# First chunks of a hop moved ahead of the last projection, and fifteen of 21 row gathers instead of ten, in a two-layer graph network on one core

## Chip, cores and metric

The kernel runs on one core of one Trainium2 chip. The metric is the device time of one launch in microseconds (us). A core has a matrix engine (PE, with its weight loads shown as PEld), a vector engine (DVE), a scalar engine (ACT), a general engine (POOL) and a queue that only starts transfers (SP). POOL starts the indirect transfers, the gathers; ACT and SP start plain ones. All numbers are float32.

## What is computed

Shapes: x is 8 batches of 2048 nodes with 128 features; adj, called R here, is a 2048 x 2048 matrix in which some 0.4% of the entries are not zero. Cut to what matters:

```python
# layer 0
res = si[:, :, None] + sj[:, None, :] + adj[None] * w_r + g_b
x = layernorm(x + einsum('bij,bjd->bid', res, x) @ weight + bias)
# layer 1: A1 = A2 = adj, so four hops come down to two
x1 = einsum('bnf,nw->bwf', x, adj)
x2 = 2 * einsum('bnf,nw->bwf', x1, adj) - x
y = relu(concat(x, x1, x2, x1, x2) @ Theta1 + bias)      # per node
x = layernorm(x + y)
```

In the kernel, layer 1 is a nested scheme over two "hops". With U = x Theta-part, hop 1 makes Y1 = x Theta-part + R^T U, and hop 2 makes x Theta-part + R^T Y1, then the relu, the residual and the layernorm.

## The kernel before, in words

**Tiling.** The 2048 nodes are 16 chunks of 128. A chunk's rows for all 8 batches are 128 x 1024 numbers (512 KB). Chunks 0 to 2 (`ND = 3`) are dense in layer 0: their product with R runs over all 16 chunks. The other 13 are sparse: of each the list of node rows that R really touches is known, and seven gathers (four lists for tiles of 32 columns, two for 64, one for 128) fetch those rows of the operand from DRAM into one of nine buffers `G`, which lie over the first nine tiles named Y (`fetch_lists`, line 736). `listed_rows` (line 886) multiplies them: eight matmuls with 32 columns of weights, four with 64 and two with 128, each written to the trace as two instructions, so 28 records a chunk. The matching rows of R are gathered by `gathers` (line 709): a small gather of 128 rows per list into one of four `stage` tiles, and `keep_r` (line 681) on DVE masks and packs a full stage. For chunks 0 to 2, which need lists in layer 1 alone, 21 such gathers (`dense_jobs = 7 * ND`) read adj itself: in the trace, `stage<-in_adj_dram,idr`. These come last in the list of jobs: four for each of chunks 0, 1, 2, then three for each.

**Order around the change.** The last part of layer 0 runs over the 13 sparse chunks, `seq` = 9 to 14, 3 to 8, and then 15 (`LAST`). In each turn PE does `listed_rows`, and `finish0` (line 379) on DVE and ACT adds the residual and takes the layernorm. `make_u` (line 388) of the chunk before runs meanwhile: 8 transposes on PE into PSUM, one copy of each half out of PSUM (DVE and ACT), 16 matmuls with Theta into two PSUM tiles of the tag "sm" (which has two buffers), two ACT copies, and one store of the chunk of U to `u_d`, issued by ACT. After the last chunk come the ten gathers of line 934, plain loads on SP (lines 937 and 939) and the `make_u` of chunk 15 (line 940). Then hop 1 starts.

**A hop** (line 942). `begin(n)` opens the accumulation of the hop's n-th chunk: 16 matmuls with x transposed (line 952) and two products with the chunk's diagonal block (line 878, 4 records), whose operand `own` and block `rd` SP has loaded. The accumulators are the two pairs of `bank` in turn, but each third chunk takes both "sm" tiles. `listed_rows` then adds the lists, `end` copies the result out and stores it. Three chunks are begun before the first `listed_rows`; from then on a chunk is begun two ahead. The first two chunks (`first`) gather from all of U but chunk 15, and take chunk 15's part by `block_rows` with a block `rl` that SP loads into the same three buffers as `rd`; the third and later gather from the whole of `u_d`. After the `listed_rows` of each chunk from the third on, hop 1 calls `gathers(2)`, until the 21 are done.

**What sets the order.** On PE, `in_order` ties each matmul of this part behind the one written before it. On POOL, `gather` (line 658) ties each gather behind the one before. SP's loads keep program order. So the order of the source is the order of these queues, and a gather that waits holds up all later ones.

Of the kernel before, what the change touches and what calls it, by code (L numbers as in the profile page):

```python
# [18 lines left out]
def kernel(  # L19
# [86 lines left out]
    def rows4(name):  # L106
        return w4.tile([P, B, D], F32, name=name, tag="w4")

    def flat(t):
        return t.rearrange("p b f -> p (b f)")  # L110
# [69 lines left out]
    def transpose4(srcs, name, t=None, dve=None, tie=None):  # L180

        pt = p_tr.tile([P, 4, P], F32, name=f"pt_{name}", tag="pt")
        for i, s in enumerate(srcs):
            mm = nc.tensor.transpose(pt[:, i, :], s, ident)  # L184
            if tie is not None:
                tie(mm)
        if t is None:
            t = trp.tile([P, 4, P], F32, name=f"tr_{name}", tag="tr")
        evict(t, pt, dve)
        return t  # L190
# [176 lines left out]
    def acc_pair():  # L367
        par[0] ^= 1
        return bank[2 * par[0]:2 * par[0] + 2]
# [18 lines left out]
    def make_u(c, z, xt, u=None, tie=None, mid=None):  # L388

        for h in range(2):  # L390
            transpose4([z[:, h * HB + i, :] for i in range(4)], f"p{c}_{h}",
                       xt[:, h * HB:(h + 1) * HB, :], tie=tie)
        if mid is not None:
            mid()
        if c < ND:
            nc.scalar.dma_start(out=xt_d[c], in_=flat(xt))
        if u is None:
            u = rows4(f"u{c}")
        for h in range(2):
            pp = p_sm.tile([P, HB, D], F32, name=f"pp{c}_{h}", tag="sm")  # L400
            for i in range(HB):
                mm = nc.tensor.matmul(  # L402
                    pp[:, i, :], xt[:, h * HB + i, :], th[:, 0, :], start=True, stop=True
                )
                if tie is not None:
                    tie(mm)
            nc.scalar.copy(u[:, h * HB:(h + 1) * HB, :], pp)  # L407
        nc.scalar.dma_start(out=u_d[c * P:(c + 1) * P, :], in_=flat(u))
# [262 lines left out]
    def gather_r(c, q, m, st, n):  # L671


        gather(
            st[:, n * m * P:(n + 1) * m * P],
            rr_d[c - ND].rearrange("n m f -> n (m f)") if m == 2 else adj128,
            idx if m == 2 else idr,
            4 * c + n if q else (LP + 2 * c, LP + 2 * c + 1, LF + c)[n], NX if m == 2 else N * NC,
        )
# [26 lines left out]
    dense_jobs = 7 * ND  # L706
    waiting = []

    def gathers(count, mm=None):

        for _ in range(count):
            if not jobs:
                break
            c, q, n = jobs.pop(0)
            if n == 0:
                if len(waiting) == 3:
                    keep_r(*waiting.pop(0))
                waiting.append((
                    c, q, int(c >= ND) + 1,
                    stages[:, turn[1] % 4 * BD:turn[1] % 4 * BD + BD + 4 * TW],  # L720
                ))
                turn[1] += 1
            gather_r(*waiting[-1], n)
            if mm is not None:
                tc.add_manual_dep(
                    order[-1].ins, mm.ins.name,
                    mybir.DependencyInfo(
                        mybir.DependencyClass.Sync, mybir.DependencyReason.DATA
                    ), reason="pace",
                )  # L730
# [78 lines left out]
    with nc.allow_non_contiguous_dma(reason="512-byte rows of blocks"):  # L809
        pending, accs, xr = None, acc0, load_x(0, "xr", nc.sync)  # L810
        for c in range(ND):
# [62 lines left out]
            pending, xr = (c, z, rows4(f"xt{c}")), xr1  # L874
# [8 lines left out]
    def own_rows(i, c, accs, start):  # L883
        block_rows(*own.pop((i, c)), accs, start, False)
# [19 lines left out]
    with nc.allow_non_contiguous_dma(reason="512-byte rows of a diagonal block"):  # L904
        def begin0(c):
            accs = acc_pair()
            own_rows(0, c, accs, True)
            if c in first:
                block_rows(Y[LAST], late0, accs, False, False)
            begun[c] = accs  # L910

        begun = {}
        xr = load_x(seq[0], "xs", nc.sync)
        begin0(seq[0])
        for c, c1 in zip(seq, seq[1:] + [None]):
            if c1 is not None:
                fetch_own(0, y0_d, c1)
                if c1 in first:
                    late0 = fetch_block(0, c1)
                xr1 = load_x(c1, "xs", nc.sync)  # L920
                put(c)
                while any(job[0] == c1 for job in jobs):
                    gathers(1)
            else:
                put(c)
            accs = begun.pop(c)
            if c == LAST:
                listed_rows(0, y0_d, c, accs, lambda: make_u(*pending, tie=in_order))
            else:
                listed_rows(0, y0_d, c, accs)  # L930
                make_u(*pending, *[None] * (4 - len(pending)), in_order, lambda: begin0(c1))
            z = finish0(c, accs, xr)
            if c == LAST:
                gathers(dense_jobs // 2)
            pending, xr = (c, z, x1t[c], held.get((1, c))), xr1
        for c in hops[:2]:
            fetch_own(1, u_d, c)
        for c in range(ND):
            fetch(xt_d[c], f"xt_{c}", x1t[c])
        make_u(*pending, tie=in_order)  # L940

        def hop(i, src):
            def begin(n):
                c = hops[n]
                if (i, c) not in own:
                    fetch_own(i, src, c)
                accs = acc_pair() if n % 3 < 2 else [
                    p_sm.tile([P, HB, D], F32, name=f"acc{i}_{c}_{h}", tag="sm") for h in range(2)
                ]
                for h in range(2):  # L950
                    for b in range(HB):
                        in_order(nc.tensor.matmul(  # L952
                            accs[h][:, b, :], x1t[c][:, h * HB + b, :], th[:, i, :],
                            start=(b == 0), stop=False, skip_group_check=True,
                        ))
                own_rows(i, c, accs, False)
                return accs

            def end(c, accs):
                z = held.get((i + 1, c)) if i == 1 else None  # L960
                if z is None:
                    z = rows4(f"z{i}_{c}")
                for h in range(2):
                    hs = slice(h * HB, (h + 1) * HB)
                    if i == 1:
                        evict(z[:, hs, :], accs[h], h == 1)
                        continue
                    pt = p_tr.tile([P, HB, P], F32, name=f"pt_r{c}_{h}", tag="pt")
                    for b in range(HB):
                        in_order(nc.tensor.transpose(pt[:, b, :], x1t[c][:, h * HB + b, :], ident))  # L970
                    nc.vector.tensor_add(z[:, hs, :], accs[h], b1bc.to_broadcast([P, HB, D]))
                    nc.vector.scalar_tensor_tensor(  # L972
                        z[:, hs, :], z[:, hs, :], 0.0, pt, op0=ALU.max, op1=ALU.add
                    )
                if i == 1:
                    nc.scalar.dma_start(out=y_d[c * P:(c + 1) * P, :], in_=flat(z))
                else:
                    layernorm(z, f"1_{c}")
                    nc.scalar.dma_start(
                        out=out[:, c * P:(c + 1) * P, :].rearrange("b p f -> p b f"), in_=z  # L980
                    )

            early = [begin(n) for n in range(3)]
            late = [fetch_block(i, c) for c in first]
            for n in range(2):
                listed_rows(i, src, hops[n], early[n])
            for n, c in enumerate(hops):
                if i == 1 and n == NC - 5:
                    while waiting:
                        keep_r(*waiting.pop(0))  # L990
                if n < 2:
                    block_rows(held[i, LAST], late[n], early[n], False, True)
                else:
                    listed_rows(i, src, c, early[n])
                    if i == 1:
                        gathers(2)
                if 1 <= n < NC - 2:
                    early.append(begin(n + 2))
                end(c, early[n])

        hop(1, u_d)
        hop(2, y_d)


# [86 lines left out]
```

## Time and profile before

| | us |
|---|---|
| runs | 852.25, 855.61, 860.12 |
| median | 855.61 |
| profiled execution, whole time | 867.91 |
| its span on the core | 866.1 |
| PE busy | 748.5 (86%) |
| POOL busy | 430.1 (50%) |
| DVE busy | 364.1 (42%) |
| ACT busy | 175.1 (20%) |
| moved by the transfers | 269.19 MB, mean 311 GB/s |

The span lies 1.8 us below its execution's own time, and that execution is 12.3 us over the median of the three runs. In the trace, layer 0 ends and hop 1 begins between about 462 and 490 us, hop 1 lasts to about 685 us, and hop 2 to the end. The page's row of DMA rates gives the share of each 1/40 of the span (21.65 us); the slices in which this border falls show 259 and 280 GB/s, those of the later part of hop 1 up to 394.

### The profile page before, as it was taken

How to read it: one execution, taken by the hardware profiler on the slowest of the kernel's cores; microseconds unless marked ns; L12 is line 12 of the kernel's file. 1: busy time of each engine (PE TensorE's matmuls, PEld its weight loads, DVE VectorE, ACT ScalarE, POOL GpSimd, SP SyncE). 2: the span in 40 equal slices, each digit the busy share in tenths (PEclk: the TensorE clock that was granted, in tenths of full speed). 3: DMA queues.
4: the chain of work that ended last, by engine and by line, in shares of the span. 5: the costliest groups of instructions: out<-in, count | busy, mean ns of one | idle time of the engine just before them, and what ended most of it. 6: DMA issues, size and time to landing. Idle time of an engine off the chain costs nothing.

```text
span 866.1 us, 10670 instructions
## 1 busy us (share of the span) xinstructions
PE 748.5 (86%) x3546; PEld 373.8 (43%) x3546; DVE 364.1 (42%) x1062; ACT 175.1 (20%) x428; POOL 430.1 (50%) x438
## 2 busy tenths in 40 slices
PE   5899999998829778498996987989999899999994
PEld 4666665643324333153344442333343444445541
DVE  5555667769523335155353010000100046555666
ACT  3665664010011212021222000000000002011111
POOL 0000000277466676657675456766655656566660
PEclk9999999999869998799998999999999999999998
DMA  8699997799968889979997889999998989999994
GB/s 283 194 306 309 342 303 215 231 373 398 287 212 264 268 274 322 368 250 344 342 363 259 280 314 349 315 341 394 383 365 307 322 290 372 350 341 354 342 350 155
DMA packets 177548, 269.19 MB, mean 311 GB/s; under 512 B 17698, under 2 KB 127701, under 8 KB 175438
## 3 DMA queue, kind: packets, MB, share of 16 engines
q0 software_dynamic: 50400, 151.21, 49.0%
q1 hardware_dynamic: 103900, 90.02, 32.0%
q10 hardware_dynamic: 23186, 27.20, 8.8%
q8 instruction: 30, 0.49, 0.2%
q14 instruction: 32, 0.26, 0.1%
HBM read 246.75 MB, written 62.55 MB: 357 GB/s over the span
## 4 chain that ended last, share of the span: by engine, by line
PE 53%; DMA 19%; issue 10%; another core or an unknown queue 8%; POOL 3%; DVE 3%; ACT 2%; POOLq 1%; SPq 0%; DVEq 0%; ACTq 0%
PE acc L894 19%; DMA Y<-u_d,idx 9%; DMA Y<-y_d,idx 9%; PE acc L862 7%; PE acc L878 5%; PE acc L342 4%; PE acc L332 4%; PE acc L952 3%; POOL Y L659 3%; PE pt_a L184 2%; PE pp L402 2%; DMA rc<-in_adj_dram 1%; PE pt_x L184 1%; PE pt_r L970 1%
## 5 line engine op out<-in xcount | busy, mean ns | idle before, releaser
L659 POOL DMA_INDIRECT Y<-y_d,idx x203 | 201.8, 994 | 134.7 <-PE acc L894 72.4
L894 PE MATMUL acc<-Y,rc 128*32 128x512 f32 (+2 forms) x896 | 222.3, 612 | 21.9 <-DMA Y<-u_d,idx 11.7
L659 POOL DMA_INDIRECT stage<-rr_d,idx x91 | 94.2, 1035 | 199.8 <-PE rank_c L514 164.4
L659 POOL DMA_INDIRECT Y<-u_d,idx x112 | 111.4, 994 | 69.8 <-PE acc L894 35.5
L894 PEld LDWEIGHTS acc<-Y,rc 128*32 128x32 f32 (+2 forms) x896 | 59.5, 129 | 174.5 <-issue 107.0
L894 PE MATMUL acc<-Y,rct 128*32 128x512 f32 (+2 forms) x364 | 106.2, 621 | 18.6 <-issue 14.0
L878 PE MATMUL acc<-Y,rd 128*128 128x512 f32 x148 | 70.0, 594 | 0.8 <-issue 0.8
L894 PEld LDWEIGHTS acc<-Y,rct 128*32 128x32 f32 (+2 forms) x364 | 25.5, 129 | 90.4 <-issue 67.5
L862 PE MATMUL acc<-Y,wide 128*128 128x512 f32 x128 | 59.9, 620 | 4.3 <-issue 4.3
L383 DVE TENSOR_TENSOR xs<-acc,xs 128x512 f32<-128x512 f32 x26 | 17.8, 684 | 103.8 <-PE acc L894 59.8
L176 DVE COPY z<-acc 128x512 f32<-128x512 f32 x9 | 6.2, 692 | 115.7 <-issue 41.0
L219 ACT ACTIVATE st<-st,epst 128x8 f32<-128x8 f32 x32 | 10.0, 311 | 210.1 <-DVE st L218 112.8
L184 PE MATMUL pt_a<-ident,rc 128*128 128x128 f32 x256 | 37.6, 282 | 6.4 <-DMA rc<-in_adj_dram 6.0
L972 DVE SCALAR_TENSOR_TENSOR z<-z,pt_r 128x512 f32<-128x512 f32 x32 | 20.5, 684 | 47.0 <-PE acc L894 28.5
L862 PEld LDWEIGHTS acc<-Y,wide 128*128 128x128 f32 x128 | 24.7, 199 | 34.5 <-issue 34.4
L311 DVE TENSOR_REDUCE stage<-rct 128x64 f32<-128x2048 f32 x13 | 29.7, 2286 | 23.1 <-ACT rct L178 23.1
L332 PE MATMUL acc<-wx,tr_x 128*128 128x130 f32 x256 | 36.5, 286 | 3.2 <-ACT tr_x L178 2.8
L303 DVE TENSOR_REDUCE rc<-rc 128x64 f32<-128x2048 f32 x16 | 36.5, 2278 | 6.3 <-DMA rc<-in_adj_dram 6.3
L332 PEld LDWEIGHTS acc<-wx,tr_x 128*128 128x128 f32 x256 | 32.8, 194 | 13.4 <-ACT tr_x L178 5.9
L184 PEld LDWEIGHTS pt_a<-ident,rc 128*128 128x128 f32 x256 | 30.9, 145 | 16.3 <-issue 14.7
L342 PE MATMUL acc<-Y,wide 128*128 128x512 f32 x64 | 36.0, 645 | 1.7 <-ACT Y L336 0.5
L407 ACT COPY u<-pp 128x512 f32<-128x512 f32 x30 | 17.5, 585 | 98.3 <-PE acc L894 58.7
(221 smaller groups left out, 895.2 us busy)
## 6 DMA issues: line engine op xcount, KB each, us to landing
rc<-in_adj_dram SPq DMA_DIRECT2D x16, 1024.0 KB
rr_d<-rct SPq DMA_DIRECT2D x13, 1024.0 KB
rr_d<-in_adj_dram SPq DMA_DIRECT2D x13, 1024.0 KB
xs<-in_x_dram SPq DMA_DIRECT2D x21, 512.0 KB
y_d<-Y SPq DMA_DIRECT2D x16, 512.0 KB
out_dram<-z ACTq DMA_DIRECT2D x16, 512.0 KB
u_d<-u ACTq DMA_DIRECT2D x15, 512.0 KB
Y<-y_d SPq DMA_DIRECT2D x15, 512.0 KB
```

The lines of the kernel that those rows point to most:

```text
L184: mm = nc.tensor.transpose(pt[:, i, :], s, ident)
L303: nc.vector.tensor_reduce(mk[:, c, :], a.rearrange("p (w f) -> p w f", f=TW), AX.X, ALU.max, apply_absolute_value=True,)
L311: nc.vector.tensor_reduce(mkt[:, :, 4 * c:4 * c + 4], at.rearrange("p j (t f) -> p j t f", f=TW), AX.X, ALU.max, apply_absolute_value=True,)
L332: nc.tensor.matmul(py[:, i, 0:D + 2], xt[b // HB][:, (b + i) % HB, :], wx, start=True, stop=True,)
L342: nc.tensor.matmul(acc0[h], first_at[0][:, c, :], Y[c][:, h * HB:(h + 1) * HB, :], start=(c == 0), stop=False, skip_group_check=True,)
L383: nc.vector.tensor_add(xr[:, hs, :], accs[h], xr[:, hs, :])
L659: g = nc.gpsimd.indirect_dma_start(out=out, out_offset=None, in_=src, in_offset=bass.IndirectOffsetOnAxis(ap=ids[:, n:n + 1], axis=0), bou ...
L862: mm = nc.tensor.matmul(accs1[h], at1[:, j, :], Y[j][:, h * HB:(h + 1) * HB, :], start=(j == 0), stop=False, skip_group_check=True,)
L878: in_order(nc.tensor.matmul(accs[h], r, t[:, h * HB:(h + 1) * HB, :], start=start, stop=stop, skip_group_check=True,))
L894: in_order(nc.tensor.matmul(accs[h][w * t:w * t + w], r[:, o + w * t:o + w * t + w], gs[t][:, h * HB * D:(h + 1) * HB * D], start=False, s ...
L952: in_order(nc.tensor.matmul(accs[h][:, b, :], x1t[c][:, h * HB + b, :], th[:, i, :], start=(b == 0), stop=False, skip_group_check=True,))
L972: nc.vector.scalar_tensor_tensor(z[:, hs, :], z[:, hs, :], 0.0, pt, op0=ALU.max, op1=ALU.add)
```

## The change

Two edits. After the last chunk of layer 0, fifteen of the 21 gathers of R for chunks 0 to 2 are issued instead of ten; the other six are left for hop 1's `gathers(2)`. And the `make_u` of chunk 15 moves into the hop: in hop 1 it is written after the `begin` of the first two chunks and ahead of the third one's. In hop 2 the three `begin` follow each other as before.

```diff
             if c == LAST:
-                gathers(dense_jobs // 2)
+                gathers(dense_jobs - 6)
             pending, xr = (c, z, x1t[c], held.get((1, c))), xr1
...
         for c in range(ND):
             fetch(xt_d[c], f"xt_{c}", x1t[c])
-        make_u(*pending, tie=in_order)
-
         def hop(i, src):
...
-            early = [begin(n) for n in range(3)]
+            early = [begin(n) for n in range(2)]
+            if i == 1:
+                make_u(*pending, tie=in_order)
+            early.append(begin(2))
             late = [fetch_block(i, c) for c in first]
```

## The prediction, made blind

> **What bounds the kernel now.** I read the page first: PE is busy for 86% of the span, and the chain of waits gives PE 53%, transfers 19%. That is an average, so I went to the border that the change touches, in the timeline of PE. Columns: start in us, duration, engine and line, operation, operands, count, and in brackets idle time and what ended it.
>
> ```profile
> 465.31 1.88 PE L894 MATMUL acc<-Y,rct 128*128 128x512 f32 x4
> 471.24 1.94 PE L184 MATMUL pt_p<-ident,xs 128*128 128x128 f32 x8 [4.05 <-issue]
> 473.11 3.74 PE L402 MATMUL pp<-th,Y 128*128 128x128 f32 x16
> 476.68 1.95 PE L952 MATMUL acc<-th,wide 128*128 128x128 f32 x16
> 478.47 1.88 PE L878 MATMUL acc<-Y,rd 128*128 128x512 f32 x4
> 480.19 1.95 PE L952 MATMUL acc<-th,wide 128*128 128x128 f32 x16
> ...
> 487.29 7.59 PE L894 MATMUL acc<-Y,rc 128*32 128x512 f32 x34
> ```
>
> After the last matmul of layer 0 (end 467.19) PE stands 4.05 us until DVE and ACT have normalized chunk 15, transposes it, makes its U, begins three chunks of hop 1, and reaches their gathered rows only at 487.29. Now the timeline of POOL:
>
> ```profile
> 466.11 1.00 POOL L659 DMA_INDIRECT stage<-in_adj_dram,idr  x1 [0.30 <-issue]
> 469.98 1.00 POOL L659 DMA_INDIRECT Y<-u_d,idx  x1 [2.87 <-DMA u_d<-u]
> ...
> 480.37 0.99 POOL L659 DMA_INDIRECT Y<-u_d,idx  x1 [0.30 <-issue]
> 489.46 0.99 POOL L659 DMA_INDIRECT Y<-u_d,idx  x1 [8.11 <-PE acc L894]
> ```
>
> POOL issues the tenth gather of R, waits 2.87 us for a store of U, fills the nine buffers at 1.30 us each, and then stands 8.11 us until PE has read a buffer. Last, the same stretches by windows (busy us of each engine, granted clock, share of the transfer engines, GB/s):
>
> ```profile
> 467.00:471.20 4.20, 0.19 (x1) 0.00 (x0) 3.68 (x19) 0.71 (x3) 1.10 (x2) 0.84 0.38 142
> 471.20:477.00 5.80, 5.76 (x27) 5.46 (x28) 1.79 (x5) 2.15 (x6) 4.50 (x5) 0.53 0.78 242
> 481.40:489.50 8.10, 8.10 (x49) 4.31 (x49) 0.00 (x0) 0.00 (x0) 0.04 (x1) 1.00 0.85 306
> 541.00:587.00 46.00, 42.22 (x177) 17.51 (x181) 2.96 (x5) 2.35 (x4) 31.92 (x32) 0.96 0.93 328
> 594.00:640.00 46.00, 42.74 (x194) 17.88 (x193) 3.96 (x10) 2.62 (x5) 28.70 (x30) 1.00 1.00 384
> ```
>
> So at this border PE, not the gathers, ends last: transfers run at 142 GB/s, later the gathers wait for PE. From 594 on, transfers are full; between 541 and 587, where five gathers of R still lie among those of U, they are not.
>
> **What the Trainium skill says.** "TensorE: Matmul & The Clock Gate", What's actually happening: after an idle window of some 3.4 us PE's clock falls to half, and it needs as long a busy one to come back. The trace agrees: after 4.05 us idle the clock is 0.53, and 16 matmuls for U take 3.74 us where those of the chunk before (463.42) took 2.05. "DMA: Bandwidth & Descriptors", Issuing engines are not separate DMA queues: all queues share 16 engines; so loads that SP starts sooner meet the gathers. Specifications there puts a core's HBM limit at 358 GB/s; the trace shows 384, and the trace decides. Anatomy of one DMA gives 2.0 us and the bytes at 436 GB/s: an estimate of 3.2 us for 512 KB. The trace has 4.4 us (469.98 to its landing mark at 474.36) to 7.7 us (480.37 to 488.05) for the nine, so I use those.
>
> **Part 1, the two begins ahead of U: PE.** Nothing is added; 40 records of PE move. One begin costs 480.19 - 476.68 = 3.5 us, two 7.0. They are ready: landing marks show both `own` rows and blocks in by 456.2; the first takes the bank pair that chunk 15 doesn't hold, the second needs `finish0`'s additions, which DVE ends at 467.99, against a start at 467.19 + 3.5 = 470.7. They end at 474.2. The norm ends on DVE at 472.30, on ACT at 472.06, so nothing is left to wait for: transposes to the last U matmul took 465.47 - 461.98 = 3.5 us for the chunk before, which ends them at 477.7. New is that `begin(2)` follows at once on the "sm" tiles that ACT empties: its second half needs the second ACT copy, some 0.7 us after the last matmul, of which its own first half (0.9 us) hides most; 0 to 0.7, I take 0.1. `begin(2)` ends at 477.7 + 0.1 + 3.5 = 481.3. PE is ready 6.0 us sooner: 4.05 of idle time and 1.95 of half clock and waits.
>
> **Part 1, the queues.** ACT's store of chunk 15's U goes from 477.50 to about 478.2; its readers are the gathers from the third chunk on (495.94), and it takes 6.5 us, so 11 us are spare: no cost. On SP the `make_u` issues nothing, but its block loads `rl` waited until 482.93 for the begins' buffers; they now start near 471 and 475, and behind them the 512 KB `own` rows of the fourth chunk (484.26) near 475, among the gathers. 640 KB at 384 GB/s is 1.7 us of shared transfer time: 0 to 1.7, I take 0.8.
>
> **Part 2, five more gathers of R: POOL.** Each is 1.30 us start to start. The tenth ends at 467.11, so the five start at 467.41 to 472.6, and the first of U at 473.93 instead of 469.98: 2.6 us lie in POOL's wait for the store, 3.95 are new. Queued behind them are all gathers of U, and PE waits for those. The new list's first gather also puts one `keep_r` on DVE (0.28 us) before the copy for U: its four gathers have landed by 465.6 and PE's transposes come at 474.2, so it costs nothing; a landing after 474 would hold up that copy.
>
> **The sum at the border.** The fourth gather starts at 477.83; with 5.55 us (as now) and the 0.8 it lands at 484.2. PE, ready at 481.3, waits for it, which is what is late next. Four tiles take 1.85 us (487.29 to 489.14), POOL follows 0.3 us later: the tenth gather of U at 486.4 instead of 489.46, a gain of 3.1 us; POOL's floor, nine gathers after 473.93, is 485.6, or 3.8. With 7.7 us of latency it is 0.9. From there gathers pace PE in both kernels (1.30 us each up to 505), so all later work shifts. Range 0.9 to 3.8, I take 3.1.
>
> **The sum later.** `gathers(2)` has 6 left instead of 11, so the five at 547.96, 549.27, 561.16, 562.47 and 572.88 are gone: 6.5 us of POOL. What they are worth depends on what fills in. If transfers do, only 320 KB at 384 GB/s, 0.9 us. If the pace becomes that of the later chunks (begins at 594.63 and 605.91: 11.3 us a chunk, against 12.2 from 545.91 to 594.63), four chunks gain 3.6; all of POOL's time would be 6.5. I take 2.2. In sum 3.1 + 2.2 = 5.3 us. Against the profiled execution that is 867.9 - 5.3 = 862.6; nothing in either term is seen to depend on what makes that execution 12.3 us longer than the median, so against the median: 850.3.
>
> **The rivals.** (a) **Larger gain**: latencies as now without the 0.8, and POOL's whole 6.5 us returned: 3.8 + 6.5 = 10.3, 845.3. For it: POOL is issuing almost back to back from 541 to 587. Against: PE needs 9.1 us a chunk (1.78 + 1.72 + 5.64 on the chain) and transfers are at 0.93. (b) **No change**: the gain at the border is taken up in the stretch of full transfers, since the bytes are the same and the loads only come sooner: 855.6 - 0.9 = 854.7. Against: transfers before that stretch were idle, so the same bytes start sooner. (c) **Slower**: the five gathers hold back the first gather of U while transfers are idle, and PE's lead turns into a wait. The deciding point is a latency L of the fourth with 477.83 + L + 1.85 + 0.3 over 489.46, L over 9.5 us. Such ones exist: 13.4 us for the gather at 446.63, in a full stretch (408 GB/s). Then the tenth starts 3.9 us late, and with nothing returned it is 859.5. Against: 4.4 to 7.7 here. A loss over 1% would need more than this. (d) **The change doesn't do what it says**: the begins are not ready at 467.2. Then PE is at the rows at 487 as before, the gathers (last of the first seven near 489) still fit, and only part 2's 2.2 is left: 853.4. The landing marks speak against it.
>
> **How the numbers follow.** The forecast (gain of 2 to 8.5 us) gets 0.57, (a) 0.18, (b) and (d) together 0.13, (c) 0.12. The time is the forecast's, 850.3. The range takes in the sum's own bounds (0.9 + 0.9 to 3.8 + 3.6), most of (a), and (b), and an uncertainty of some 2 us in the medians: 844 to 857. One per cent is 8.6 us, about what a measurement of this kernel can tell from no change. Faster by more: (a)'s upper part and the edge of the forecast, 0.20. Slower by more: (c) with something beside it, 0.10. Within: 0.70.
>
> **What would show it.** PE without a wait of 4 us after layer 0, with `begin` records between the last layer 0 matmul and the transposes; the granted clock there near 1.0; the 16 U matmuls at about 2.05 us; the first gather of U 3.9 us after where it was relative to layer 0's end, the nine at once, and POOL's 8.11 us gone; begins in mid-hop nearer 11.3 than 12.2 us. The prediction is wrong if PE's wait for the fourth gather is over 5 us, if `begin(2)` waits over 1 us for the ACT copies, or if the lead of the tenth gather is seen but not the shift at hop 2's start.

## The result and the profile after

| | before | after | ratio, 95% interval |
|---|---|---|---|
| median of 20 runs each, us | 859.24 | 865.24 | 1.0062 [1.0036, 1.0089] |
| lowest to highest, us | 852.25 to 866.30 | 855.82 to 869.75 | |
| span of the profiled execution, us | 866.1 | 867.5 | |

The change cost 6.0 us by these medians, where a gain of 5.3 was forecast. The ratio leaves out the runs over 1.5% above the fastest of their kernel, four of the 20 after the change, and comes to some 5.3 us of loss. The profile shows where the forecast broke in one execution. First the timeline of PE after the change (start, duration, engine, line, operation, operands, count; in brackets the idle time and what ended it):

```profile
463.89 1.88 PE L894 MATMUL acc<-Y,rct 128*128 128x512 f32 x4
465.61 1.95 PE L950 MATMUL acc<-th,wide 128*128 128x128 f32 x16
...
472.61 1.04 PE L184 MATMUL pt_p<-ident,xs 128*128 128x128 f32 x8
486.91 3.78 PE L402 MATMUL pp<-th,Y 128*128 128x128 f32 x16 [13.27 <-DVE Y L176]
490.49 3.03 PE L950 MATMUL acc<-th,wide 128*128 128x128 f32 x16
...
495.17 5.28 PE L894 MATMUL acc<-Y,rc 128*32 128x512 f32 x27
```

Down to 472.61 this is the forecast: both begins stand directly behind layer 0's last matmul, and the wait of 4.05 us is gone. Then PE stands 13.27 us for DVE's copy of the transposed chunk. DVE's timeline says what the copy waited for:

```profile
470.67 0.29 DVE L687 TENSOR_TENSOR rc<-stage,has 128x128 f32<-128x128 f32 x1
486.17 0.69 DVE L176 COPY Y<-pt_p 128x512 f32<-128x512 f32 x1 [15.21 <-remote]
```

The packing of the new list (line 687) is over at 470.96, as forecast. The transposes are on record as ended at 473.65, yet the copy starts at 486.17, and its releaser is not PE but "remote": no record near 486 carries the semaphore that released it. The chain of waits in this stretch calls the same time an unknown queue (start, length, what):

```profile
470.76 0.20 DVE rc L687
470.96 15.22 another core or an unknown queue
486.18 0.69 DVE Y L176
```

There is one core. The semaphore's own marks settle what came late: PE's completion mark for the first begin lies at 476.79, where its last record ends at 469.27; that of the second begin lies at 486.01, recorded end 472.77; the eight transposes follow at 486.04 to 486.28. So PE's matmuls finished, as far as any other engine could see, up to 13.2 us after their records. The Trainium skill, "Perfetto Trace Analysis", Per-engine timelines, says that a matmul's reported end is computed from its size, and that the semaphore is pushed only after PSUM has acknowledged the data. This trace agrees, with 12.5 us between the two for the transposes. SP saw the same marks: its two loads of `rl` need the buffers that the two begins free, and the first went out at 476.81, the second at 486.03:

```profile
476.81 9.55 SPq L795 DMA_DIRECT2D rl<-in_adj_dram  x2
```

The granted clock was 0.61 from 472.60 to 486.90:

```profile
463.90:472.60 8.70, 8.70 (x46) 5.79 (x45) 5.50 (x23) 2.16 (x5) 6.57 (x8) 1.00 0.35 112
472.60:486.90 14.30, 1.05 (x9) 0.80 (x7) 0.69 (x1) 0.59 (x1) 8.59 (x9) 0.61 0.80 268
486.90:495.20 8.30, 8.29 (x40) 7.05 (x41) 0.00 (x0) 1.17 (x2) 0.00 (x0) 0.65 0.42 144
```

(busy us of PE, its weight loads, DVE, ACT and POOL, then clock, share of the transfer engines, GB/s). The stretch that should have started the rows early moves 144 GB/s, because POOL has filled its nine buffers and PE reads none. The extra gathers of R are not what is late here: the ninth gather of U had landed by 488.4, while PE comes to the rows at 495.17.

```profile
482.64 0.99 POOL L659 DMA_INDIRECT Y<-u_d,idx  x1 [0.31 <-issue]
497.35 0.99 POOL L659 DMA_INDIRECT Y<-u_d,idx  x1 [13.71 <-PE acc L894]
```

In the first kernel's profile the same thing was there to be read, a little further on. Its chain of waits has, in the first chunks of hop 1:

```profile
472.36 0.69 DVE Y L176
473.06 35.60 another core or an unknown queue
508.65 0.02 issue
```

and its page puts 8% of the span down to "another core or an unknown queue". The 35.60 us are DVE's whole stand, not the delay: the matmuls whose result it copies at 508.68 end on record between 503.1 and 505.7, so 3 to 5.6 us of it are late finish. Counted over the whole trace, 79 of the 628 marks of PE on record came over 1 us after the record before, the latest by 17.6 us; after the change 88 of 632, the latest by 16.5. The kernel has 730 such marks, so both traces lack some 100 of them.

Between the two profiles the parts are: before layer 0's last matmul -1.4 us; from there to the first listed rows of hop 1 ("the border" below) 21.98 before and 31.28 after, +9.3; from those rows to hop 2 183.58 and 178.20, -5.4; hop 2 -1.1. In sum +1.4, as the spans say. These are two single executions, 8.7 and 4.2 us over their kernels' medians, so the pair shows a wait at the border and not the loss of 6.0.

### The profile page after: what moved, and what is told of

Its sections match the earlier page's. It is cut to its first block, busy times and chain, and to the rows that moved or that the text cites. A ratio compares the mean times of both kernels' runs of the same rounds, so it can differ in the third digit from the quotient of the medians.

```text
span 867.5 us, 10674 instructions
## 1 busy us (share of the span) xinstructions
PE 744.5 (86%) x3546; PEld 374.1 (43%) x3546; DVE 364.4 (42%) x1062; ACT 175.1 (20%) x428; POOL 429.3 (49%) x438
## 4 chain that ended last, share of the span: by engine, by line
PE 42%; DMA 26%; issue 13%; another core or an unknown queue 6%; DVE 5%; ACT 3%; POOL 3%; SPq 1%; POOLq 1%; DVEq 0%; ACTq 0%
PE acc L894 15%; DMA Y<-u_d,idx 12%; DMA Y<-y_d,idx 9%; PE acc L878 5%; PE acc L342 4%; PE acc L332 4%; PE acc L950 3%; POOL Y L659 3%; PE acc L862 2%; PE pt_a L184 2%; PE pp L402 2%; DVE rc L569 2%; DMA rct<-xt_d 1%; DMA rc<-in_adj_dram 1%
## 5 line engine op out<-in xcount | busy, mean ns | idle before, releaser
L894 PE MATMUL acc<-Y,rct 128*32 128x512 f32 (+2 forms) x364 | 102.6, 633 | 18.2 <-DMA Y<-y_d,idx 14.1
L862 PEld LDWEIGHTS acc<-Y,wide 128*128 128x128 f32 x128 | 24.3, 194 | 28.3 <-issue 28.3
L950 PEld LDWEIGHTS acc<-th,wide 128*128 128x128 f32 x256 | 32.3, 198 | 7.5 <-issue 7.5
```

The costliest lines, as they stand in the source:

```text
L862: mm = nc.tensor.matmul(accs1[h], at1[:, j, :], Y[j][:, h * HB:(h + 1) * HB, :], start=(j == 0), stop=False, skip_group_check=True,)
L894: in_order(nc.tensor.matmul(accs[h][w * t:w * t + w], r[:, o + w * t:o + w * t + w], gs[t][:, h * HB * D:(h + 1) * HB * D], start=False, s ...
L950: in_order(nc.tensor.matmul(accs[h][:, b, :], x1t[c][:, h * HB + b, :], th[:, i, :], start=(b == 0), stop=False, skip_group_check=True,))
```

## Experiments

Each ratio is to the kernel before on the same chip. Borders come from each run's profile. The runs fell on three other chips, where the kernel before takes 830.59, 830.75 and 829.47 to 830.05 us instead of 859.24, and where PE has no late mark at this border and the chains name no unknown queue among their larger entries.

**The parts, and two variants.** The new order alone, with ten gathers, is the diff's second edit. Fifteen gathers alone is its first:

```diff
-                gathers(dense_jobs // 2)
+                gathers(dense_jobs - 6)
```

One begin ahead of U instead of two (ten gathers):

```diff
-        make_u(*pending, tie=in_order)
...
-            early = [begin(n) for n in range(3)]
+            early = [begin(0)]
+            if i == 1:
+                make_u(*pending, tie=in_order)
+            early += [begin(n) for n in (1, 2)]
```

And the transposes first, then the two begins, then the matmuls for U (ten gathers), so that no begin stands ahead of the transposes:

```diff
-        make_u(*pending, tie=in_order)
...
-            early = [begin(n) for n in range(3)]
+            early = []
+            if i == 1:
+                make_u(*pending, tie=in_order,
+                       mid=lambda: early.extend(begin(n) for n in range(2)))
+            early += [begin(n) for n in range(len(early), 3)]
```

The new order alone:

> The reorder alone, ten gathers as before. Theory 1 (the two begins ahead of the transposes hold up the marks by which PE tells that the transposes are done, so that the copies for U come late): the copies of chunk 15 again start over 8 us after the transposes are on record, from the last layer 0 matmul's start to the first listed rows of hop 1 takes 28 us or more (before 22, after 31), and the time is 5 to 9 us above before (ratio 1.006 to 1.010), since the return in mid-hop is missing. Theory 2 (the five gathers hold up the start of hop 1): the border is shorter than before's 22 us and the time is 3 to 6 us below before (0.993 to 0.997).

Fifteen gathers alone:

> The fifteen gathers alone, U of chunk 15 ahead of the begins as before. Theory 1: the border stays at 22 us within 2, hop 1 from the first listed rows to hop 2's first begin is 2 to 6 us shorter than before's 183.6, ratio 0.993 to 0.998. Theory 2: the border is 26 us or more and the ratio 1.003 or above.

One begin ahead:

> Ten gathers, and only the first begin ahead of U of chunk 15; it fills the 4 us in which PE waited for the norm. Theory 1: one begin's delay is left, the copies come about half as late as with two (5 to 8 us), ratio 1.000 to 1.006. Theory 2: like the reorder alone but with a smaller gain, 0.995 to 1.000.

Begins between transposes and U:

> Ten gathers, transposes of chunk 15 first, then two begins, then its U. Theory 1: the transposes are told at once, the copies start within 2 us of them and run beside the begins, the border is 19 to 22 us, ratio 0.995 to 1.000. Theory 2: the same, since no gather is added. If a wait of 8 us stands at the copies here too, the order of begins and transposes is not its cause.

| kernel | us | ratio, 95% interval | border, us |
|---|---|---|---|
| new order, ten gathers | 830.22 | 1.0001 [0.9984, 1.0018] | 15.64 |
| fifteen gathers, old order | 830.73 | 1.0001 [0.9982, 1.0020] | 21.03 |
| one begin ahead | 830.16 | 0.9997 [0.9983, 1.0011] | 16.50 |
| begins between | 832.11 | 1.0028 [1.0011, 1.0045] | 21.14 |

Neither part loses anything here, so both explanations that I had then fell: that begins ahead of the transposes always hold up their marks, and that the five gathers cost. The new order does at this border just what was forecast. Of the four expected ratios only that of one begin ahead took in what was measured. The begins between transposes and U shorten nothing (21.14), because the wait of 4.05 us for the norm stays; why they lose 0.28% is not shown.

**The change itself, on another chip.** The next four were the kernel before once more (which shows what no change looks like), the change, and the two parts.

> The kernel before, unchanged, for a profile on the chip of this call. Theory 3 (the loss comes from matmuls that finish later than their records say, which is a property of the chip that a run falls on, not of the kernel): if the time is near 855 to 860 us, copies and stores that wait for PE show waits of 10 us and more put down to an unknown queue, in layer 0 too; if it is near 830, none of those waits is over 3 us and the border is 20 to 23 us. Rival: the waits come from the kernel's order and are there at either time.

> The change itself. Theory 3: on a chip with times near 830 us the copies for U of chunk 15 start within 1.5 us of the transposes, the border is 16 to 19 us, the ratio 0.996 to 1.001; on a chip with times near 858 us the copies come 8 us or more late and the ratio is 1.003 to 1.009. Rival (the two parts together lose, wherever they run, though neither does alone): ratio 1.003 or above at either time, and the first gather of U over 4 us later than with the reorder alone while PE waits for it over 4 us.

> The reorder alone again, beside the change. Theory 3: near 830 us as before (ratio 0.998 to 1.002, border 15 to 17 us); near 858 us late copies and a ratio of 1.002 to 1.009. Rival: no loss at either time.

> The fifteen gathers alone again. Theory 3: border within 2 us of the kernel before's on the same chip, ratio 0.995 to 1.002 at either time, since nothing of PE is moved. Rival: no loss at either time.

| kernel | us | ratio, 95% interval | border, us |
|---|---|---|---|
| kernel before, again | 831.31 | 1.0006 [0.9983, 1.0030] | 21.90 |
| the change | 828.73 | 0.9974 [0.9955, 0.9993] | 15.64 |
| new order, ten gathers | 831.79 | 0.9997 [0.9971, 1.0022] | 15.64 |
| fifteen gathers, old order | 829.74 | 0.9982 [0.9962, 1.0001] | 20.91 |

The same change gains 2.0 us on this chip. PE's timeline of it:

```profile
431.94 1.88 PE L894 MATMUL acc<-Y,rct 128*128 128x512 f32 x4
433.65 1.95 PE L950 MATMUL acc<-th,wide 128*128 128x128 f32 x16
...
440.66 1.04 PE L184 MATMUL pt_p<-ident,xs 128*128 128x128 f32 x8
442.04 2.05 PE L402 MATMUL pp<-th,Y 128*128 128x128 f32 x16 [0.35 <-DVE Y L176]
...
447.58 1.36 PE L894 MATMUL acc<-Y,rc 128*32 128x512 f32 x4
450.26 1.04 PE L894 MATMUL acc<-Y,rc 128*32 128x512 f32 x2 [1.32 <-DMA Y<-u_d,idx]
```

The copy waits 0.35 us instead of 13.27, the matmuls for U take 2.05 at full clock, and PE then waits for gathers. Why the 6.3 us are worth so little is seen in the gathers of U. Issue and landing marks, in us after the start of layer 0's last matmul:

| gather | before: issued, landed | change: issued, landed | landed sooner |
|---|---|---|---|
| 1st | 8.1, 12.5 | 8.2, 12.9 | -0.4 |
| 7th | 15.9, 24.5 | 16.0, 25.7 | -1.2 |
| 10th | 24.1, 31.1 | 21.9, 30.7 | 0.4 |
| 14th | 29.3, 36.2 | 27.1, 35.7 | 0.5 |
| 21st | 38.9, 45.1 | 38.5, 44.7 | 0.4 |

The tenth gather starts 2.2 us sooner, lands 0.4 us sooner, and spends the rest under way: 8.8 us of latency instead of 7.0. From the tenth on, both kernels' gathers land some 1.26 us apart. Transfers are no longer full then: between the landings of the tenth and the 21st they move 283 GB/s with the change and 301 without, at 0.85 and 0.87 of their engines' time. What the lead meets are the nine gathers ahead of the tenth, which POOL issued within 0.2 us of the same times in both: the ninth lands at 28.3 with the change and 28.6 without, and the tenth 2.4 and 2.5 us behind it. For most of the time that those nine were under way transfers were full. By windows, first the change, then the kernel before on this chip, each from 16 us after that matmul (columns as above):

```profile
447.94:455.94 8.00, 5.01 (x18) 0.80 (x16) 0.00 (x0) 0.00 (x0) 4.76 (x5) 1.00 1.00 387
```

```profile
449.86:457.86 8.00, 8.00 (x49) 4.32 (x49) 0.00 (x0) 0.00 (x0) 2.83 (x3) 1.00 1.02 384
```

Transfers are full in both here, with PE at work for 5.0 of 8 us in one and for all 8 in the other. So the lead turns into PE's waits for gathers, and the fourth chunk is begun 41.6 us after layer 0's last matmul with the change, 42.1 without.

The five extra gathers of R are covered. POOL's timeline of the kernel before on this chip, and of the change:

```profile
433.61 0.99 POOL L659 DMA_INDIRECT stage<-in_adj_dram,idr  x1 [0.30 <-issue]
441.95 0.99 POOL L659 DMA_INDIRECT Y<-u_d,idx  x1 [7.34 <-PE pt_p L184]
```

```profile
438.41 1.00 POOL L659 DMA_INDIRECT stage<-in_adj_dram,idr  x1 [0.30 <-issue]
440.17 0.99 POOL L659 DMA_INDIRECT Y<-u_d,idx  x1 [0.76 <-DMA rl<-in_adj_dram]
```

POOL waits 7.34 us in one and 0.76 in the other, and the first gather of U starts 8.1 and 8.2 us after that matmul. The names in brackets are not what it waited for: in both it starts 0.86 us after the last landing mark (7.23 and 7.37) of the store of the U of the chunk before, whose rows it reads. What they save comes back later: at the 49th gather of U, fifteen gathers (alone or with the new order) are at 85.8 to 86.1 us on this chip, ten at 88.8 to 89.2.

**A hold-up made on purpose.** If a late finish between the begins and the copies is what lost the time, a hold-up of the same length must lose it on a chip that has no late finish. The second begin's matmuls with x transposed were made eight times over in the changed kernel (the first seven results are overwritten), and in another run four times:

```diff
-                for h in range(2):
+                for h in (0, 1) * (8 if i == 1 and n == 1 else 1):
```

Beside the longer one ran one begin ahead with fifteen gathers, the change, and fifteen gathers alone; beside the shorter one the two parts.

Eight times over:

> The change, but with the 16 matmuls of the second begin with x transposed made eight times over (the first seven are overwritten), so that PE reaches chunk 15's transposes some 7 x 1.8 = 12.6 us later, about as late as the marks of these transposes came in the profile after the change (12.5 us). Theory 'late finish': a hold-up of that length between the begins and the copies is enough for the measured loss: the border from the last layer 0 matmul to the first listed rows is near 15.6 + 12.6 = 28.2 us on a chip whose marks are on time, 6.3 over the kernel before, the tenth gather of U starts some 6 us later than before relative to layer 0's end, and of this 3 to 6 us come through to the end: ratio 1.003 to 1.007. Rival 'slack': as the lead of 6.3 us was taken up within three chunks of full transfers, so is a lag of 6.3; then the ratio is 0.997 to 1.001 and the loss on the first chip came from somewhere else.

One begin ahead with fifteen gathers:

> Candidate for the best version: one begin ahead of U instead of two, fifteen gathers. Ten gathers with one begin ahead gave a border of 16.5 us, 0.9 more than two. If what is gained comes from the five gathers that leave the middle of hop 1 and the border's lead is absorbed, this equals the change: ratio 0.996 to 1.000 to the kernel before where the marks are on time, border 16.5 us. Where PE's marks come late by 12 us after long runs of matmuls, one begin fewer ahead of the transposes leaves less to be held up: ratio below the change's by 0.002 or more there.

The change, and fifteen gathers alone:

> The change once more beside the two above. Marks on time (before near 830 us): border 15.6 us, copies of chunk 15 within 1 us of its first transposes, ratio 0.996 to 0.999. Marks late (before near 859 us): border 25 us or more, copies 5 to 15 us after the transposes on record, ratio 1.002 to 1.009. The first chip's loss is reproduced only in the second case.

> Fifteen gathers without the new order. Marks on time: border 21 us, ratio 0.996 to 1.000, so that the gain of the whole change is that of this part. Marks late: ratio 0.996 to 1.001, against 1.006 for the change, if the loss belongs to the begins that stand between the last layer 0 matmul and the transposes.

Four times over, and the two parts beside it:

> As the run with the second begin's matmuls made eight times over, but four times: 3 x 1.8 = 5.4 us between the begins and chunk 15's transposes. The border is near 15.6 + 5.4 = 21.0 us, 0.9 under the kernel before. Theory 'a lead is absorbed, a lag is not': a border no longer than before's costs nothing, so this stands where fifteen gathers alone stand, ratio 0.996 to 1.000, and the whole loss of the longer hold (1.0086) belongs to the part of it that goes past the old border. Rival 'every microsecond of PE counts': it loses 5.4 us to the change, ratio 1.003 to 1.005.

> The new order alone, ten gathers. Marks on time (before near 830 us): border 15.6 us, ratio 0.998 to 1.002. Marks late (before near 850 us or more): if the loss on the first chip came with the begins ahead of the transposes, the border is 25 us or more and the ratio 1.003 to 1.011, most or all of the change's 1.0062.

> Fifteen gathers alone, old order. Marks on time: border 21 us, ratio 0.996 to 1.001. Marks late (before near 850 us or more): 0.995 to 1.002 if the first chip's loss came with the begins, 1.004 to 1.009 if it came with the gathers.

| kernel | us | ratio, 95% interval | border, us |
|---|---|---|---|
| change, begin eight times | 836.58 | 1.0086 [1.0057, 1.0116] | 28.15 |
| one begin ahead, fifteen gathers | 830.02 | 1.0000 [0.9981, 1.0018] | 16.72 |
| the change | 828.09 | 0.9979 [0.9961, 0.9997] | 15.64 |
| fifteen gathers, old order | 829.77 | 0.9990 [0.9968, 1.0012] | 20.86 |
| change, begin four times | 831.27 | 1.0013 [0.9996, 1.0031] | 21.00 |
| new order, ten gathers | 830.75 | 1.0012 [0.9995, 1.0029] | 15.65 |
| fifteen gathers, old order | 829.67 | 0.9993 [0.9973, 1.0014] | 22.46 |

With the longer hold-up PE runs on without a gap and the copies are 12.5 us late because the matmuls really take that long:

```profile
439.91 14.45 PE L950 MATMUL acc<-th,wide 128*128 128x128 f32 x128
454.20 1.88 PE L878 MATMUL acc<-Y,rd 128*128 128x512 f32 x4
455.92 1.04 PE L184 MATMUL pt_p<-ident,xs 128*128 128x128 f32 x8
457.30 2.05 PE L402 MATMUL pp<-th,Y 128*128 128x128 f32 x16 [0.35 <-DVE Y L176]
...
462.83 7.37 PE L894 MATMUL acc<-Y,rc 128*32 128x512 f32 x34
```

POOL then does what it did on the first chip, nine gathers and a stand:

```profile
453.05 0.99 POOL L659 DMA_INDIRECT Y<-u_d,idx  x1 [0.30 <-issue]
465.01 0.99 POOL L659 DMA_INDIRECT Y<-u_d,idx  x1 [10.98 <-PE acc L894]
```

The loss is 836.58 - 830.05 = 6.5 us to the kernel before, where the first chip lost 6.0; the expected ratio, 1.003 to 1.007, was a little low. It speaks against the rival that a lag is absorbed as the lead was. The shorter hold-up puts the border back to 21.0 us and lies at 1.0013, just outside what the theory expected (0.996 to 1.000) and below its rival (1.003 to 1.005). Against the change (0.9979) 5.4 us of hold-up cost some 0.34% of 830 = 2.8 us, about half; the further 7.2 us up to the longer one cost 0.73%, or 6.1, most of it. The intervals are wide, some 0.7 to 4.9 us for the first (an estimate from those of the two ratios), and that of the shorter hold-up overlaps that of fifteen gathers alone. In these runs a lead is mostly absorbed and a lag past the old border mostly paid.

No version ran faster than the change on these chips. One begin ahead with fifteen gathers is 1.0000 where the change is 0.9979, with overlapping intervals.

## Why the prediction was wrong

The time on record was 850.3; measured were 865.2. Of the 14.9 us, 3.6 are the kernel before itself, whose median was 855.61 in three runs and 859.24 in twenty. The rest, 11.3, is the effect: -5.3 forecast, +6.0 measured by the medians.

**The step that failed**, in the one execution that was profiled after the change, is PE's at the border. "They are ready" held, and so did "the norm ends on DVE at 472.30, on ACT at 472.06, so nothing is left to wait for", in the sense of inputs. But "transposes to the last U matmul took 465.47 - 461.98 = 3.5 us for the chunk before, which ends them at 477.7" took the ends of PE's records for the moment at which DVE and ACT may read. On that chip they differ, here by 12.5 us; the same stretch took from 472.61 to 490.69, 18 us. The old order has the norm's wait of 4 us between layer 0's matmuls and the transposes. The new one has 40 records of full PE work there, whose late finish fell straight on the copies that all of hop 1 waits for. That such a hold-up is enough for the loss is shown by the run with the begin made eight times.

**What is not shown.** That the delay falls here in every execution on the first chip, and so that it is the cause of the loss measured there, is not shown. Chance is the rival, since the delays change from execution to execution where the program does not. In layer 0, whose order on PE the change leaves as it was, ACT's copy of one chunk's transposes started 4.9 us after their last recorded end in the trace before (320.07, 324.96) and 18.2 us after it in the trace after the change (319.04, 337.19); for a later chunk it was the other way round, 13.4 us (353.10, 366.50) and 1.3 us (358.99, 360.33). Each of the two profiles has three delays over 10 us within the kernel; only after the change does one lie at the border.

**A clue was passed over.** The prediction said that "nothing in either term is seen to depend on what makes that execution 12.3 us longer than the median", and read PE 53% and transfers 19% from the chain without asking what the 8% of an unknown queue could be on one core. The steps of that share end at late marks of PE, and the border's term depends on when such marks come. The clue was even at the border itself, in the matmuls that the change moves: the prediction notes that the loads of `rl` "waited until 482.93 for the begins' buffers", but the first begin's last record ends at 480.35.

```profile
482.93 1.28 SPq L795 DMA_DIRECT2D rl<-in_adj_dram  x2
```

The mark came at 482.91, 2.56 us late, and nothing there was seen to wait for it but these loads.

**Where the marks come on time, each step can be judged by itself.** There too the gain of 5.3 was not reached: the change measured some 2 us.

- Two begins of 3.5 us ahead of U, clock at 1.0, matmuls for U at 2.05, `begin(2)` without a wait: right. Border 15.64; the forecast meant 481.3 - 465.31 = 16.0.
- Five gathers of R: the first of U was to start 3.95 us later. There it starts no later (8.1 and 8.2), since POOL waits that long anyway for the store. On the first chip that store had landed at 3.81, the gather went out at 4.67 before and 8.36 after, so 3.7 us later, and right.
- The tenth gather of U sooner by 3.1: measured 2.2. The fourth gather, put at 5.55 + 0.8 us under way, took 8.4 with the change; the trace from which 5.55 was read has 7 of that gather's 16 landing marks. And "from there gathers pace PE in both kernels (1.30 us each up to 505), so all later work shifts" failed. It took the times at which POOL issues for those at which PE can read. What counts is the landing, and it came nearly at the same time in both: 0.4 us sooner for the tenth, 0.5 for the fourteenth. This is rival (b), which the prediction set aside because "transfers before that stretch were idle": they were not full (197 GB/s before, 211 with the change) in the first 16 us after layer 0's last matmul, but full in the next 8 us, in both kernels alike.
- The later 2.2 us for five gathers gone from mid hop: the 49th gather comes 3 us sooner, and over three chips and four runs fifteen gathers alone measure 0.9982 to 1.0001. A fraction of the 2.2 reaches the end. The change as a whole gives 0.9974 and 0.9979, about 2 us; more than either part alone, with intervals that overlap.

The "slower" rival (c) had the right shape, a lead that becomes a wait of PE while transfers are idle, and the wrong place: it looked for a late gather, and the first chip had a late copy.

**Open:** what makes PE's completions late on the first chip, and whether the new order brings on the wait or met it by chance. The load of the transfers does not tell: over the six longest delays the share of their engines ran from 0.58 to 1.08. The two traces with late marks are also the two that lack many records, of gathers' landings more than half; whether the recording has a part in the delays is not shown. None of the later runs fell on a chip with late marks, so which part of the change loses there was not tried directly.

## What to carry to other kernels

A matmul's end in the profile is computed, and in one trace here the completion came up to 17.6 us later. Before work is put ahead of a PSUM copy, look at when the copy really started after earlier matmuls, and follow up every "remote" or unknown releaser on a one-core program. Where a fixed set of buffers is filled under full transfers, price a lead by when the gathers land, not by when they are issued: here 6.3 us of PE were worth 0.4 us at the landing. And a lead and a lag need not be priced alike: here most of the first was absorbed, and most of the second, past the old border, was paid.

## What the runs showed of the hardware

- The same one-core kernel took 859.24 us on one chip and 829.5 to 830.8 on three others. Most of the difference lies ahead of this border: layer 0's last matmul starts at 465.31 on the first, at 433.86 on another.
- PE's semaphore marks came up to 17.6 us after the records' ends on the first chip. In traces from the other chips only two or three marks come over 0.3 us late, all at the very end of the kernel. The first chip's two traces hold 628 and 632 of PE's 730 marks and 2499 and 2571 of the gathers' 6832 landing marks, the others at least 729 and 6815.
- A store of 512 KB of U, from its issue to its last landing mark, took 2.9 us on the first chip and 6.4 and 6.6 us on another.
- Gathers landed 1.26 us apart while 283 to 301 GB/s moved in all, so each brought less than its full 512 KB (at most some 0.38 MB, an estimate from these figures). An 8 us window moved 387 GB/s; the Trainium skill, "DMA: Bandwidth & Descriptors", Specifications, has 358 for a core's HBM, as half of what two cores share. This program ran on one core, and the measurement decides.
